# Reordering the first loads and the first turned weights of a two-layer graph kernel

## The chip, the core and the metric

The kernel runs on one core of one Trainium2 chip. Its time is the device time of one execution in microseconds (us). Three runs of the kernel before have a median of 1569.89 us (1569.67 to 1571.18). A separate, profiled execution gives the trace that is read here. The engines are called PE (the matrix engine), ACT (ScalarE), DVE (VectorE), POOL (GpSimd) and SP (the engine that issues most of the transfers).

## The reference, cut to what matters

Two layers work on x (4096 rows of 512 numbers) and an adjacency matrix of 4096 by 4096 with few ones.

```python
# layer 0
keep = (A > 0) & (cumsum(A > 0, axis=1) <= 64)
nb_mean = (keep @ x) / max(cnt, 1)
xj = leaky_relu(nb_mean @ W_nb.T + b_nb)
xi = leaky_relu(x @ W_line.T + b_line)
x = layernorm(x + xi + where(cnt > 0, xj, 0))
# layer 1
Wh = x @ W + bW
e = leaky(Wh @ a1 + b1 + (Wh @ a2 + b2).T);  e = where(A > 0, e, -9e15)
x = layernorm(x + softmax(e) @ Wh)
```

Only the two maps of layer 0, x by `W_nb` and x by `W_line`, and the folding of `W` with `a1` and `a2` have to do with the change.

## The kernel before

x is cut into 32 blocks of 128 rows. In layer 0 the kernel first makes the two maps of every block: `y = x @ W_nb.T`, which is stored in two parts, `y_hi` and `y_lo`, whose sum is y, and the line `x @ W_line.T + b_line`, which goes back to memory as `own_d`. Then one long loop (L723 to L750) multiplies the adjacency by all of y, and layer 1 follows (L1052 on). The order of the instructions on each engine is the order in which the program is written; each engine works through its own list, and a wait in it holds up everything behind it on that engine.

[...]both operands of a map have to be turned first. There are two ways of turning:

- `turn_by_pe` (L307) copies a 128 by 512 piece on DVE (L310) into one of four buffers `t`, lets PE turn it in four transposes (L153) into one of two PSUM buffers `pt`, and ACT copies the result to SBUF (L154). Block 0 of x and both weights go this way. A weight is turned in four parts of 128 of its output columns; part c fills columns 128c to 128c+127 of `w_t[name]`.
- Every other block of x is loaded by `load_turned_x` (L293) in four transfers on POOL's queue, with its 32 by 32 squares already in place, and DVE then turns each square (L325). The loads use three buffers `late[i % 3]`, so the load of block i + 3 waits for the turn of block i. The result lies in one of three `xt` buffers, or in room set aside for it.

`linear` (L368) makes one map of one block: four matmuls of 512 columns, each of which appears in the trace as two. `spin` (L353) issues transposes of the identity whose result nobody reads; they only keep PE busy.

The start of the program (L422 to L440) loads block 0 of x, the two weights, the line's bias, `W` and the rows `a1`, `a2`, `bW` on SP's queue, and two parts of `W_nb` on ACT's. It spins, turns block 0 and `W_nb`, makes the first map of block 0, turns `W_line`, makes the second map of block 0 and turns block 1 of x. From L494 the blocks come in pairs: sums and differences of the four pieces of the turned weights (`t1`, `t2`, `t4`, and `w12`, which is overwritten by `t3`) and of the turned x (`sums_x`) let `seven` (L533) make seven products instead of eight. Between the first map of block 0 and the first product of `seven` stand the steps that the prediction speaks of, in this order on DVE: the turn of block 2 (L494), `t1` and `t2` (L495, L496), the turn of block 3 into `x_low[1]`, a fourth `xt` buffer and so the one of block 0 again (L500), `y_low` of block 0 (L501), `line(0)` (L502), the sums (L508), `y_low` of block 1 (L510), `line(1)` (L512), `t4` and `t3` (L514, L515). ACT makes `y_hi` and the bend (Prelu) of each line, and before the loop of pairs it copies the bias into the PSUM bank of block 0's line (L589), into which the second product of the first `seven` adds.

The first `seven` (g = 1) also folds the weights: `fold_w` (L383) multiplies `W` and `bW` by the rows `a1` and `a2` and sums them, ten instructions on DVE spread over its four steps. From g = 2 on its steps hold the adjacency: `edge` on ACT (L175) and the scan on DVE (L193 to L206).

The buffers in which the raw weights are loaded are those in which the adjacency is worked on later: `nb` and `line` lie in the two `a` buffers, `W` in the two `left`, the rows in the two `edge`.

Of the kernel before, what the change touches and what calls it, by code (L numbers as in the profile page):

```python
# [9 lines left out]
F32 = mybir.dt.float32  # L10
# [10 lines left out]
P = 128  # L21
# [11 lines left out]
def two_layer_adj_gnn(  # L33
# [16 lines left out]
    nc = tc.nc  # L50
    N, C = x.shape
    NB = N // P
    NC = C // P
# [54 lines left out]
    late = [rows.tile([P, C], F32, name="c") for _ in range(3)]  # L108
# [28 lines left out]
    with ExitStack() as l0:  # L137
# [11 lines left out]
        def transpose_to(dst, src_of, n):  # L149

            pt = ps_s.tile([P, n, P], F32, name="pt")
            for k in range(n):
                nc.tensor.transpose(pt[:, k, :], src_of(k), ident)  # L153
            nc.scalar.copy(dst, pt)  # L154
# [128 lines left out]
        with ExitStack() as la:  # L283
            work = la.enter_context(tc.tile_pool(name="l0_work", bufs=2))
            wp = la.enter_context(tc.tile_pool(name="l0_w", bufs=1))
# [3 lines left out]
            w_t = {}  # L289
            xrs, xbs, xts, pys, pls = {}, {}, {}, {}, {}  # L290
            lines = {}

            def load_turned_x(i):  # L293

                if i < NB:
                    xrs[i] = late[i % 3].rearrange("p (j c) -> p j c", c=P)
                    for n in range(NC):
                        nc.gpsimd.dma_start(
                            xrs[i][ts(n, SQ)],
                            x_blk(i)[:, ts(n, P)].rearrange("(j a) c -> a j c", a=SQ),  # L300
                        )
# [5 lines left out]
            def turn_by_pe(dst, src):  # L307

                t = work.tile([P, C], F32, name="t", bufs=4)
                nc.vector.tensor_copy(  # L310
                    t.rearrange("p (m n b) -> p m n b", m=NC, b=SQ),
                    src.rearrange("p (n m b) -> p m n b", m=NC, b=SQ),
                )
                transpose_to(dst, lambda m: t[:, ts(m, P)], NC)

            def xt_tile():
                return work.tile([P, NC, P], F32, name="xt", bufs=3)

            def turn_x(i, t=None):
                if i < NB:  # L320
                    xts[i] = xt_tile() if t is None else t
                    if i == 0:
                        turn_by_pe(xts[i], xbs[i])
                    else:
                        nc.vector.transpose(  # L325
                            xts[i].rearrange("p m (j a) -> p j m a", a=SQ),
                            xrs.pop(i).rearrange("p j (m b) -> p j m b", b=SQ),
                        )
# [7 lines left out]
            raw = {}  # L336
# [12 lines left out]
            def load_w(name, src, queues):  # L349
                for c in range(NC):  # L350
                    queues[c % len(queues)].dma_start(raw[name][c], src[ts(c, P), :])

            def spin(n):  # L353

                idle = ps_acc.tile([P, P], F32, name="acc")
                for _ in range(n):
                    nc.tensor.transpose(idle, ident, ident)  # L357

            def turn_w(name, idle=0):

                wt = wp.tile([P, NC, C], F32, name=f"wt_{name}")
                for c in range(NC):
                    if idle:
                        spin(idle)
                    turn_by_pe(wt[:, :, ts(c, P)], raw[name][c])
                w_t[name] = wt

            def linear(lhs_t, name, bank=None):  # L368
                pl = ps_acc.tile([P, C], F32, name="acc") if bank is None else bank
                for k in range(NC):  # L370
                    nc.tensor.matmul(  # L371
                        pl, lhs_t[:, k, :], w_t[name][:, k, :],
                        start=(k == 0), stop=(k == NC - 1),
                    )
                return pl

            def load_rows(queue):
                for k, src in enumerate((a1, a2, b_w)):
                    queue.dma_start(early_rows[k], src.partition_broadcast(P))
                queue.dma_start(b12[:, 0:1], b1.partition_broadcast(P))  # L380
                queue.dma_start(b12[:, 1:2], b2.partition_broadcast(P))
# [33 lines left out]
            def y_terms(i, src):  # L415

                nc.scalar.copy(y_hi[i], src)
                return lambda: nc.vector.tensor_tensor(
                    y_lo[i], src, y_hi[i].bitcast(F32), ALU.subtract
                )  # L420

            load_own_x(0, nc.sync)  # L422
            load_w("nb", w_nb, (nc.scalar, nc.sync))
            load_turned_x(1)
            load_w("line", w_line, (nc.sync,))
            nc.sync.dma_start(bias_line, b_line.partition_broadcast(P))
            load_w("w", w, (nc.sync,))
            load_rows(nc.sync)
            load_turned_x(2)
            load_turned_x(3)  # L430
            spin(12)


            turn_x(0)
            turn_w("nb", 2)
            pys[0] = linear(xts[0], "nb")
            turn_w("line")
            pls[0] = linear(xts.pop(0), "line")
            turn_x(1)
            load_turned_x(4)  # L440

            wide = [pls[0]]

# [51 lines left out]
            tt(t1, w12, w11, ALU.subtract)  # L495
            tt(t2, w22, t1, ALU.subtract)  # L496
            y_low = y_terms(0, pys[0])
            pys[1] = linear(xts[1], "nb")
            x_low[1] = xt_tile()
            turn_pair(1, 1)  # L500
            y_low()  # L501
# [88 lines left out]
            idle = [lambda: None] * 4  # L590
# [80 lines left out]
        start = done[0]  # L671
# [51 lines left out]
        for s in range(NB * NS):  # L723
            i, g = divmod(s, NS)
# [14 lines left out]
            for k in range(KB):  # L739
                j = g * KB + k  # L740
                for term in (y_hi, y_lo):
                    nc.tensor.matmul(  # L742
                        accs[i], kt[:, k // 2, k % 2, :], term[j],
                        start=(j == 0 and term is y_hi),
                        stop=(j == NB - 1 and term is y_lo),
# [16 lines left out]
    wp = tile_p("l1_w", 3)  # L762
# [38 lines left out]
    x1ts, x1rows, pws, nats, wts, parts = {}, {}, {}, {}, {}, {}  # L801
# [232 lines left out]
    cnt, idle = cnts[:, 0, :], cnts[:, 1, :]  # L1034
# [17 lines left out]
    for s in range(NS):  # L1052
# [13 lines left out]
        k = s - FIRST  # L1066
# [13 lines left out]
        if s in range(FIRST + 14, FIRST + 22, 2):  # L1080
            q, part = divmod((s - FIRST - 14) // 2, 2)
# [5 lines left out]
    for q in range(NP * NT):  # L1087
        g, k = divmod(q, NP)
# [99 lines left out]
```

## Time and profile before

| | |
|---|---|
| median of three runs | 1569.89 us (1569.67 to 1571.18) |
| the profiled execution's own time | 1572.24 us |
| its span, first to last instruction | 1570.4 us |
| PE busy | 1559.4 us (99%) |
| DVE busy | 1258.5 us (80%) |
| ACT busy | 952.6 us (61%) |
| POOL busy | 241.2 us (15%) |
| first map's matmuls begin | 11.68 us into the span |
| first `seven`'s second product begins | 30.81 us into the span |

Times inside the profile are microseconds from the start of the span. A line of the chain of work reads: start, length, engine or transfer, tile and source line, count. A line of the timeline reads: start, length, engine, source line, operation, output and inputs, count, and in brackets how long the engine stood idle before and what ended that. L153 and L154 are the lines of a helper that every turned piece shares. A busy PE in the table counts matmuls whose ends are modelled.

### The profile page before, as it was taken

The page shows a single profiled execution, that of the slowest core. Times are in us where ns is not written, and L with a number is a line of the kernel's source. Part 1 is how long each engine was busy: PE and PEld are TensorE (multiplying, and loading weights), DVE is VectorE, ACT ScalarE, POOL GpSimd, SP SyncE. Part 2 cuts the span into 40 slices and gives each one's busy share as a digit, 9 for nine tenths or more (in the row PEclk, how much of TensorE's full clock was granted, in tenths as well). Part 3 has the DMA queues.
Part 4 walks back from the last instruction along what each step waited for, and adds up shares of the span by engine and source line. Part 5 has one row for each costly group of instructions (what it writes and reads, how often), then busy time and mean ns, then how long its engine had stood idle before and what let it go on. Part 6 is the DMA issues. An engine that isn't in the chain of part 4 may idle for free.

```text
span 1570.4 us, 18598 instructions
## 1 busy us (share of the span) xinstructions
PE 1559.4 (99%) x6408; PEld 1211.5 (77%) x6408; DVE 1258.5 (80%) x2306; ACT 952.6 (61%) x1123; POOL 241.2 (15%) x397
## 2 busy tenths in 40 slices
PE   8999999999999999999999999999999999999998
PEld 5444468888888888854488888888888888888887
DVE  5888658999999998447888888788878878888765
ACT  2676558887888878417065675556765557655530
POOL 4454212222122122120000000000000000000000
PEclk9999999999999999999999999999999999999999
DMA  7766468889888987653111111111111111111101
GB/s 234 201 203 208 160 166 265 258 250 258 242 260 222 265 253 209 147 120 113 50 41 41 28 54 53 43 48 27 48 54 41 54 34 35 55 41 54 42 1 40
DMA packets 170430, 193.01 MB, mean 123 GB/s; under 512 B 101424, under 2 KB 134480, under 8 KB 162144
## 3 DMA queue, kind: packets, MB, share of 16 engines
q1 hardware_dynamic: 147968, 131.38, 29.2%
q0 software_dynamic: 21792, 59.53, 13.3%
q8 instruction: 50, 0.82, 0.2%
q10 hardware_dynamic: 576, 0.92, 0.2%
q14 instruction: 44, 0.36, 0.1%
HBM read 132.91 MB, written 42.08 MB: 111 GB/s over the span
## 4 chain that ended last, share of the span: by engine, by line
PE 97%; DVE 1%; DMA 1%; ACT 0%; issue 0%; POOL 0%; POOLq 0%; DVEq 0%; ACTq 0%
PE acc L970 35%; PE acc L742 30%; PE pt L970 14%; PE acc L489 8%; PE acc L1056 7%; PE acc L371 3%; PE pt L371 0%; PE pt L153 0%; DMA c<-in_x_dram 0%; DVE edge L386 0%; DMA xb<-in_x_dram 0%; DVE left L194 0%; ACT edge L175 0%; PE acc L357 0%; ACT wt_line L154 0%
## 5 line engine op out<-in xcount | busy, mean ns | idle before, releaser
L970 PE MATMUL acc<-bt,s 128*128 128x256 f32 x1504 | 335.7, 379 | 0.0
L742 PE MATMUL acc<-y_hi,kt 128*128 128x512 f32 x824 | 320.5, 389 | 0.0
L742 PE MATMUL acc<-y_lo,kt 128*128 128x512 f32 x824 | 320.5, 389 | 0.0
L970 PEld LDWEIGHTS acc<-bt,s 128*128 128x128 f32 x1504 | 285.8, 190 | 38.9
L855 ACT ACTIVATE w<-nat,few 128x1024 f32<-128x1024 uint8 x128 | 136.9, 1137 | 293.3 <-DVE a L930 238.8
L970 PE MATMUL acc<-bt,a 128*128 128x256 f32 x1056 | 239.0, 379 | 0.0
L970 PE MATMUL pt<-bt,a 128*128 128x256 f32 x992 | 224.5, 379 | 0.0
L970 PEld LDWEIGHTS acc<-bt,a 128*128 128x128 f32 x1056 | 200.6, 190 | 27.3
L970 PEld LDWEIGHTS pt<-bt,a 128*128 128x128 f32 x992 | 188.5, 190 | 26.1 <-issue 0.5
L930 DVE STREAM_TRANSPOSE a<-w 128x1024 f32<-128x1024 f32 x128 | 153.1, 1225 | 62.0 <-ACT w L911 53.2
L277 ACT ACTIVATE kt<-ktb,few 128x1024 fp32r<-128x1024 uint8 x124 | 142.7, 1152 | 97.8 <-PE acc L742 80.1
L126 POOL TENSOR_TENSOR rs<-ve,few 128x1 f32<-128x1 f32 x64 | 46.8, 731 | 940.3 <-DVE ve L124 927.6
L742 PEld LDWEIGHTS acc<-y_lo,kt 128*128 128x128 f32 x824 | 154.7, 188 | 32.2
L742 PEld LDWEIGHTS acc<-y_hi,kt 128*128 128x128 f32 x824 | 154.6, 188 | 32.1
L848 ACT ACTIVATE w<-w,st_n 128x1024 f32<-128x1024 f32 x128 | 149.4, 1234 | 33.3 <-DVE m L865 33.3
L911 ACT ACTIVATE w<-w,nm 128x1024 f32<-128x1024 f32 x128 | 145.4, 1138 | 11.1 <-DVE nm L902 11.1
L865 DVE CUSTOM_DVE_ANT_0 w<-e_n,w 128x1024 f32<-128x1024 f32 x128 | 149.4, 1220 | 1.8 <-ACT w L855 0.5
L175 ACT ACTIVATE edge<-a,few 128x2048 bf16<-128x2048 int32 x64 | 136.2, 2128 | 6.3 <-issue 2.7
L223 ACT CAST code<-left 128x2048 uint8<-128x2048 bf16 x64 | 121.2, 1893 | 0.0
L1056 PE MATMUL acc<-w,c 128*128 128x512 f32 x232 | 99.7, 592 | 0.0
L1056 PEld LDWEIGHTS acc<-w,c 128*128 128x128 f32 x232 | 44.1, 190 | 55.5 <-issue 53.8
L206 DVE TENSOR_TENSOR left<-edge,left 128x2048 bf16<-128x2048 bf16 x64 | 78.4, 1225 | 2.2
(188 smaller groups left out, 1904.5 us busy)
## 6 DMA issues: line engine op xcount, KB each, us to landing
a<-in_adj_dram SPq DMA_DIRECT2D x64, 1024.0 KB, 5.9
code_d<-code POOLq DMA_DIRECT2D x64, 256.0 KB, 4.0
nat<-code_d SPq DMA_DIRECT2D x256, 64.0 KB, 2.0
w<-x_d SPq DMA_DIRECT2D x128, 64.0 KB, 2.0
c<-in_x_dram POOLq DMA_DIRECT2D x124, 64.0 KB, 5.2
own<-in_x_dram SPq DMA_DIRECT2D x31, 256.0 KB, 3.2
own<-own_d POOLq DMA_DIRECT2D x31, 256.0 KB, 5.5
x_d<-own POOLq DMA_DIRECT2D x31, 256.0 KB, 4.8
```

The costliest lines, as they stand in the source:

```text
L175: nc.scalar.activation(edge_of[s], loaded.pop(s).rearrange("p (t q) -> p q t", q=2), AF.Sigmoid, bias=steep[:, 0:1], scale=STEEP, accum_ou ...
L223: nc.scalar.copy(code.bitcast(U8).rearrange("p (t q) -> p q t", q=2), seen_of.pop(s))
L277: nc.scalar.activation(kts[s], bytes_.rearrange("p t (i r) -> p t r i", r=2), AF.Sigmoid, bias=steep[:, 1:2], scale=STEEP,)
L489: nc.tensor.matmul(bank, lhs[:, k, :], rhs[:, k, :], start=start and k == 0, stop=k == 1, skip_group_check=True,)
L742: nc.tensor.matmul(accs[i], kt[:, k // 2, k % 2, :], term[j], start=(j == 0 and term is y_hi), stop=(j == NB - 1 and term is y_lo),)
L848: nc.scalar.activation(dst, src, AF.Prelu, bias=bias, scale=scale, alpha=0.2)
L855: nc.scalar.activation(wts[b][:, i, :], nats[b, i // 2].bitcast(U8)[:, i % 2, :], AF.Relu, bias=far, scale=-FAR,)
L865: nc.vector.tensor_tensor_reduce(w_i, e2_n, w_i, 1.0, -3e38, ALU.subtract, ALU.max, m4s[b][:, i : i + 1])
L911: nc.scalar.activation(w_i, w_i, AF.Exp, bias=nms[b][:, i : i + 1], accum_out=z4s[g][:, r, i : i + 1])
L930: nc.vector.transpose(a[:, r].rearrange("p s (i a) -> p i s a", a=SQ), wts[2 * g + r][:, :, ts(k, 8 * SQ)].rearrange("p i (s x) -> p i s x ...
L970: nc.tensor.matmul(banks[g][n], lhs[:, j, :], bt[:, 4 * k + j, rhs, :], start=(k == 0 and j == 0 and n == mate[0]), stop=(k == NP - 1 and ...
L1056: nc.tensor.matmul(pws[s], x1t[:, m, :], ws[:, m, :], start=(m == 0), stop=(m == NC - 1))
```

## The change

The order of the first loads changes. Block 1 of x moves from POOL's queue to SP's, between `W_nb` and `W_line`. `W_line` is issued by ACT and SP in turn, as `W_nb` was. Blocks 2 and 3 of x, and `W` with the rows, are issued later in the program, each group behind a memset on DVE that writes one column of its first buffer: the transfer writes the same column and so has to wait for the memset, and the memset stands on DVE behind the copies of `W_nb`, or behind the turn of block 1. There are 15 spins ahead of the first turn instead of 12.

The first map of block 0 is made in two pieces: columns 0 to 383 first, columns 384 to 511 after two parts of `W_line` have been turned. Both pieces add into the same PSUM bank. Then the other two parts of `W_line` are turned. After that comes the map of block 1 by `nb`, and only then the map of block 0 by `line`. Before, block 0's `line` map came first, and block 1's `nb` map stood after `t1`, `t2` and `y_terms(0, ...)` in the program.

```diff
-            def load_turned_x(i):
+            def load_turned_x(i, queue=nc.gpsimd):
...
-                        nc.gpsimd.dma_start(
+                        queue.dma_start(
...
-            def turn_w(name, idle=0):
-
-                wt = wp.tile([P, NC, C], F32, name=f"wt_{name}")
-                for c in range(NC):
+            def turn_w(name, idle=0, parts=range(NC)):
+
+                if name not in w_t:
+                    w_t[name] = wp.tile([P, NC, C], F32, name=f"wt_{name}")
+                for c in parts:
                     if idle:
                         spin(idle)
-                    turn_by_pe(wt[:, :, ts(c, P)], raw[name][c])
-                w_t[name] = wt
-
-            def linear(lhs_t, name, bank=None):
+                    turn_by_pe(w_t[name][:, :, ts(c, P)], raw[name][c])
+
+            def linear(lhs_t, name, bank=None, part=slice(0, C)):
+
                 pl = ps_acc.tile([P, C], F32, name="acc") if bank is None else bank
                 for k in range(NC):
                     nc.tensor.matmul(
-                        pl, lhs_t[:, k, :], w_t[name][:, k, :],
-                        start=(k == 0), stop=(k == NC - 1),
+                        pl[:, part], lhs_t[:, k, :], w_t[name][:, k, part],
+                        start=(k == 0 and part.start == 0),
+                        stop=(k == NC - 1 and part.stop == C),
+                        skip_group_check=part.stop - part.start < C,
                     )
                 return pl
...
             load_own_x(0, nc.sync)
             load_w("nb", w_nb, (nc.scalar, nc.sync))
-            load_turned_x(1)
-            load_w("line", w_line, (nc.sync,))
+            load_turned_x(1, nc.sync)
+            load_w("line", w_line, (nc.scalar, nc.sync))
             nc.sync.dma_start(bias_line, b_line.partition_broadcast(P))
+            spin(15)
+
+
+            turn_x(0)
+            turn_w("nb", 2)
+
+            for i in (2, 3):
+                nc.vector.memset(late[i % 3][:, 0:1], 0.0)
+                load_turned_x(i)
+            pys[0] = linear(xts[0], "nb", part=slice(0, 3 * P))
+            turn_w("line", 0, range(0, 2))
+            linear(xts[0], "nb", pys[0], slice(3 * P, C))
+            turn_w("line", 0, range(2, 4))
+            turn_x(1)
+            load_turned_x(4)
+            nc.vector.memset(raw["w"][0][:, 0:1], 0.0)
             load_w("w", w, (nc.sync,))
             load_rows(nc.sync)
-            load_turned_x(2)
-            load_turned_x(3)
-            spin(12)
-
-
-            turn_x(0)
-            turn_w("nb", 2)
-            pys[0] = linear(xts[0], "nb")
-            turn_w("line")
+            pys[1] = linear(xts[1], "nb")
             pls[0] = linear(xts.pop(0), "line")
-            turn_x(1)
-            load_turned_x(4)
...
             y_low = y_terms(0, pys[0])
-            pys[1] = linear(xts[1], "nb")
             x_low[1] = xt_tile()
```

## The prediction

> **What bounds the kernel now.** First the page's chain of work that ended last, by engine:
>
> ```profile
> PE 97%; DVE 1%; DMA 1%; ACT 0%; issue 0%; POOL 0%; POOLq 0%; DVEq 0%; ACTq 0%
> ```
>
> The matrix engine (PE) is nearly the whole chain, so only its idle stretches can be won or lost. The chain in order of time says where they are:
>
> ```profile
> 51.34 122.27 PE acc L489 x284
> ```
>
> From 51.34 us on PE runs without a gap, so what the change does before that comes out as a shift of all that follows. I then read the chain of the first 56 us:
>
> ```profile
> 0.74 3.74 DMA xb<-in_x_dram
> ...
> 10.37 0.64 PE pt L153 x4
> 11.02 0.02 issue
> 11.04 0.59 ACT wt_nb L154
> 11.63 0.04 issue
> 11.68 3.70 PE acc L371 x8
> ...
> 17.18 1.09 ACT wt_line L154 x2
> 18.27 0.04 issue
> 18.31 3.71 PE acc L371 x8
> 22.02 0.02 issue
> 22.05 0.72 DVE xt L325
> ...
> 50.67 0.62 DVE acc L574
> 51.29 0.04 issue
> ```
>
> Block 0 of x (`xb`) lands at 4.48; the turn of `nb` runs on PE to 11.0. Twice PE then stands until ScalarE (ACT) has copied the last turned part of a weight, 0.67 us before 11.68 and 0.68 before 18.31. From 22.05 VectorE (DVE) carries the chain. The chain shows a DMA of x at 24.68 to 29.48, but the instruction behind it (L514) reads no x and stands directly behind L402 on DVE, so I take that step for a coincidence. The timeline gives the rest:
>
> ```profile
> 1.37 2.82 PE L357 MATMUL acc<-ident 128*128 128x128 f32 x12 [1.37 <-POOL ident masks.py:199]
> 4.99 1.12 PE L153 MATMUL pt<-ident,t 128*128 128x128 f32 x4 [0.80 <-DVE t L310]
> 15.21 1.04 PE L153 MATMUL pt<-ident,t 128*128 128x128 f32 x8
> 28.91 0.69 DVE L402 TENSOR_TENSOR t<-acc,bias_line 128x512 f32<-128x512 f32 x1 [2.12 <-PE acc L371]
> 30.81 3.70 PE L489 MATMUL acc<-hi,lo 128*128 128x512 f32 x8 [0.22 <-ACT acc L589]
> ```
>
> L402 at 28.91 is `line(1)`, the bias added to the second map of block 1. It waits for PE. Behind it DVE works without a pause to 42.9, then comes the first `edge` on ACT and its scan, up to the product at 51.34. So **the start of line(1) sets 51.34**, and with it the end.
>
> **The change, part by part.**
>
> Loads up to the first map. ACT issues four transfers instead of two. At 0.45 each (two took 0.90) they end near 2.6; its table load (1.28) then ends near 3.9 instead of 2.95, under the wait for the first copy at 6.14. Price 0; if ACT's issues had to wait, each us past a table end of 6.1 would be lost. SP issues `xb`, two parts of `nb`, four of x block 1, then `line` parts 1 and 3, bias. SP's seventh issue before (4.68) stood until `xb` had landed at 4.48, so `line` part 3, ninth in its queue, goes out near 5.9. The data up to it is 2.62 MB; 0.56 MB came before 4.0 us and 335 GB/s followed from 4 to 8, so it lands near 10.2 (before: 13.1). The last `nb` part landed at 7.37 (issue 1.67, 5.7 to landing). Its new neighbour on the engines is a part of `line` instead of x from POOL; even at 8.5 it stays ahead of its turn near 9.7. Price 0.
>
> Three more spins: at the pitch of the cold turn, 0.2133 (four take 0.85), they end at 4.19 + 0.64 = 4.83, before the first turn at 4.99. Price 0.
>
> [...]The clock column shows 1.00 in all these windows, so I read the rate from durations: four transposes take 0.85 from 5 to 10 us, eight take 1.04 at 15.21, and the x4 at 10.37 takes 0.64, that is two at 0.213 and two at 0.107. Full rate began near 10.8. [...] The longer spin cuts the 0.80 gap to 0.16. [...] I take 0, the nearer row, and keep 1.7 as a rival.
>
> The interleaving. Before, PE's way from the turn of `nb` to line(1): first matmul at 11.68, `pls[0]` ends 22.02. After, the first three quarters of block 0's map need only turned parts 0 to 2, and the third was copied by 10.57, so PE goes on at about 10.95. A 512-column matmul has two records 0.43 apart, so eight at 3/4 length take 2.58: 13.53. Two parts of `line` turned, 8 transposes at 0.107: 14.39. The last quarter, 8 records of 128 columns: between 0.107 (columns alone, or the transposes' pitch) and 0.190 (if the weight load of 190 ns cannot overlap); I take 0.115, near the transposes, whose loads overlap too: 0.92, 15.31 (bounds 0.86 and 1.52). Two more parts: 16.17; their PSUM buffers are free, since copies of 0.59 follow transposes that ended at 13.96 and 14.39. Then block 1 by `nb`, 3.44: 19.61, which covers the copy of the last `line` part (PE waited 0.68 for it before). Then block 0 by `line`: 23.05, with 0.26 of drain 23.3.
>
> This is 1.3 **later** than 22.02, and it matters: the turn of block 3 into `x_low[1]` takes the third-next `xt` buffer, that of block 0, and waits for this map. From that turn's start to line(1) DVE needs, by the starts before, 0.63 + 0.58 + 0.60 (turn, y_low, line(0)), three sums to 3.01, and 0.69 for y_low(1), plus about 0.1 as ACT's conversion for it ends 3.1 after the turn's start: 3.8. So line(1) starts at 27.1. PE ends the fourth map at 23.05 + 3.44 + 0.26 = 26.75 and is no longer what it waits for. Gain 28.91 − 27.1 = **1.8** (1.2 to 1.9 by the bounds of the last quarter). PE follows: 1.90 lay between line(1) and the product at 30.81 (bias, Prelu and a copy on ACT), so 29.0.
>
> Moved loads. Two memsets on DVE behind the last `nb` copy (7.9) release POOL at 8.1 for x blocks 2 and 3: 8 issues of 0.55, last at 12.0, at most 7.5 us to landing for such before: 19.5. Block 3 is wanted at 23.3; cover 3.8. Block 2 lands near 16.5, ahead of `t1`, which needs `line` copied near 16.9. Blocks 4 and 5 queue on POOL behind them and their own turns: landed by 27, wanted at 30 and 32. Block 6 goes out 1.3 later than at 23.05, landing near 30.8, wanted at 42.81 − 1.8. The third memset, behind the turn of block 1 (12.2), releases SP for `w`, the rows, then adjacency. That is 6.3 later than 5.93: a2 landed at 19.35, now 25.7, and the first fold wants it at 32.42 − 1.8 = 30.6; cover 4.9. Adjacency 0 landed at 27.1, now 33.4, wanted at 43.1. The memsets cost some 0.1 in DVE time where it waits anyway. All 0 while the covers hold.
>
> **Sum.** The profiled execution: 1572.24 (span 1570.4 and 1.84 around it) − 1.8 = 1570.4. The runs' median is 1569.89; the same shift gives **1568.1**.
>
> **Rivals.**
>
> A. As summed: 1568.1, own range 1567.4 to 1569.0. Chance 0.52.
>
> B. [...]1568.1 − 1.7 = 1566.4, with 1565.7 to 1567.2. [...] DVE and loads would follow: block 3 would be wanted at 21.6, `line` part 3 near 13. Chance 0.26.
>
> C. The gain is hidden: x block 3 lands late. Its landing at 23.3 + 1.8 would bring line(1) back to 28.91: 1569.9. A time of 10.9 to landing, the longest of its kind, gives 22.9, so it needs a slower one still, beside `w` and rows released in the same us. Or the chain at 24.68 was real after all. Chance 0.14.
>
> D. Slower: the fold weights come too late. DVE reaches the first fold at 30.6 with everything of the chain behind it. Up to 4.9 of lateness is covered; the next 1.8 eat the gain; to be slower by 3.1 takes a2 landing after 35.5, 23 us after the release instead of 13.4. With twice the old 13.4 it lands at 39.1, DVE stands 8.5, and the time is 1576.6. For it: these ten transfers now start together with x blocks 2 to 5. Against: `line` is done by then, and before they shared the engines with it. Chance 0.08.
>
> **How the numbers follow.** 0.2% is 3.1 us, about what this kernel's measurement can tell. Faster by more needs a time under 1566.75: about three quarters of B and 0.02 from elsewhere, 0.22. Slower: most of D and a remainder, 0.07. The rest, 0.71, is within. The range 1565.9 to 1570.5 holds A, nearly all of B and most of C, and leaves out D.
>
> **What would show it.** Right: no wait of PE for ACT between 11 and 18; the map of block 1 by `nb` ahead of block 0 by `line`; line(1) near 27.1 waiting for no PE; the unbroken run of PE from near 49.5. B: the transposes of `nb` part 2 at 0.107 apart. C: the turn of block 3 waits for a DMA. D: a fold waits for a DMA near 30.6. Wrong in a way not listed: the quarter of 128 columns takes over 1.5, or ACT's first copy is later than 6.14.

## The result, and the profile after

The changed kernel takes 1567.92 us (median of 14 runs, 1567.17 to 1568.77); 14 runs of the kernel before beside it take 1571.37 (1569.67 to 1572.42). The ratio is 0.998, with a 95% interval of 0.9972 to 0.9988: faster by 0.2%, 3.1 us by the ratio and 3.45 by the medians. The forecast time, 1568.1, is close, and the forecast range holds the measured one, but the forecast started from three runs with a median of 1569.89, lower than that of the 14. The gain is nearly twice the 1.8 us of the sum.

The page's chain of work by engine, of the kernel after:

```profile
PE 98%; DVE 1%; issue 0%; ACT 0%; DMA 0%; POOLq 0%; DVEq 0%; ACTq 0%
```

The chain of the first 56 us, of the kernel after (start, length, engine, tile and line; `linear` is L372 now, the products of `seven` are L498):

```profile
...
6.50 0.85 PE pt L153 x4
7.35 0.32 PE acc L357 x2
7.67 0.44 PE pt L153 x4
...
8.76 0.22 PE acc L357 x2
8.98 0.46 PE pt L153 x4
9.44 2.85 PE acc L372 x8
12.29 0.87 PE pt L153 x8
13.16 0.89 PE acc L372 x8
14.05 0.87 PE pt L153 x8
14.93 6.88 PE acc L372 x16
21.81 0.02 issue
21.83 0.71 DVE xt L325
...
47.26 0.62 DVE acc L582
47.88 0.04 issue
```

Both waits of PE for ACT are gone: from the turn of `nb` to the end of block 0's `line` map no other engine stands in the chain. The long chain of the same kernel:

```profile
47.92 122.15 PE acc L498 x284
```

The unbroken run starts at 47.92 instead of 51.34. The timeline of the kernel after:

```profile
1.37 3.46 PE L357 MATMUL acc<-ident 128*128 128x128 f32 x15 [1.37 <-POOL ident masks.py:199]
4.95 1.12 PE L153 MATMUL pt<-ident,t 128*128 128x128 f32 x4
...
7.51 0.60 PE L153 MATMUL pt<-ident,t 128*128 128x128 f32 x4
...
25.50 0.68 DVE L405 TENSOR_TENSOR t<-acc,bias_line 128x512 f32<-128x512 f32 x1
...
25.64 1.98 PE L498 MATMUL acc<-wt_nb,xt 128*128 128x512 f32 x4 [0.41 <-DVE y_lo L421]
```

The spins now reach almost to the first turn, and from near 7.4 us the transposes of `nb` take half the time (in the chain above four take 0.85 at 6.50 and 0.44 at 7.67). So PE's first map starts at 9.44. In the profile before the turn ended at 11.0 and the map started at 11.68. `line(1)` (now L405) has no wait in its row and starts at 25.50 instead of 28.91.

The accounts of the two profiled executions agree. Span 1570.4 to 1566.6 is 3.8. Of this, 3.41 is there at line(1): 11.0 − 9.44 = 1.56 from the clock, as PE's rate, read from these durations, is called below, and 1.85 from the order. The run of PE starts 3.42 earlier; its last matmul ends 3.57 earlier (1562.48 and 1558.91 in the chains), and the last transfer brings the other 0.2.

### The profile page after: what moved, and what is told of

Read it like the earlier page. It is cut to its first block, busy times and chain, and to the rows that moved or that the text cites. A ratio compares the mean times of both kernels' runs of the same rounds, so it can differ in the third digit from the quotient of the medians.

```text
span 1566.6 us, 18624 instructions
## 1 busy us (share of the span) xinstructions
PE 1557.8 (99%) x6419; PEld 1211.5 (77%) x6419; DVE 1258.2 (80%) x2309; ACT 952.7 (61%) x1123; POOL 238.4 (15%) x393
## 4 chain that ended last, share of the span: by engine, by line
PE 98%; DVE 1%; issue 0%; ACT 0%; DMA 0%; POOLq 0%; DVEq 0%; ACTq 0%
PE acc L978 35%; PE acc L750 30%; PE pt L978 14%; PE acc L498 8%; PE acc L1064 7%; PE acc L372 3%; PE pt L372 0%; PE pt L153 0%; DVE edge L389 0%; DMA xb<-in_x_dram 0%; DVE left L194 0%; ACT edge L175 0%; DVE y_lo L421 0%; DVE xt L325 0%; ACT L175 0%
```

## The experiments

All times are medians. Each group of four ran on one chip beside the kernel before, which took 1572.43 in the first group, 1572.48 in the second and 1572.76 in the third. That is 1.1 to 1.4 above the runs of the result, for changed kernel and old alike. So I compare differences to the before of the same group.

### Theories

Theory 1: the order of turns and maps gives 1.8 us and the clock, through the spins, the rest. Its rivals: the order gives all and the spins do nothing; or the loads are the gain.

### 1. The kernel before with 15 spins

```diff
-            spin(12)
+            spin(15)
```

> The kernel before with 15 spins in place of 12, nothing else. Theory 1 (the clock): of the 3.45 us between the medians 1571.37 and 1567.92 some 1.7 are the clock, which opened near 7.4 us in the changed kernel's profile and near 10.7 in the profile before; the three spins close the gap of 0.8 us ahead of the first turn and alone bring this. Then this kernel takes about 1569.8, and its second and later nb turns run at a pitch of 0.107 us. Rival (the order alone): [...]the spins do nothing, and this kernel takes 1571.4, as before.

1571.15, which is 1.28 under before (ratio 0.9993, 0.9985 to 1.0001). The interval just includes no change; the spread says more. All 13 executions lie within 1570.93 to 1571.72, while the 57 of before lie between 1570.28 and 1573.56. The timeline of this kernel shows the turn of `nb` at the full pitch from its first part, four transposes in 0.60 (1.06 at 6.33 in the profile before):

```profile
6.27 0.60 PE L153 MATMUL pt<-ident,t 128*128 128x128 f32 x4
...
27.03 0.69 DVE L402 TENSOR_TENSOR t<-acc,bias_line 128x512 f32<-128x512 f32 x1 [2.13 <-PE acc L371]
```

line(1) still waits 2.13 for PE, as before, and starts 1.88 earlier than there. The expected 1.6 is not reached in the median, perhaps because some executions of before reach the full rate early too; none of them was profiled, so this is not shown (experiment 2 has such an execution of the changed kernel).

### 2. The changed kernel with 12 spins

```diff
-            spin(15)
+            spin(12)
```

> The changed kernel with the 12 spins of before. Theory 1 (the clock): the gap of 0.8 us is back, [...]and 1.2 to 1.7 us of the gain go: about 1569.4. Rival (the order alone): 1567.9, unchanged.

1570.06, 2.37 under before (0.9987, 0.998 to 0.9993). The 21 executions fall into two groups with nothing between: 8 from 1568.37 to 1569.14, 13 from 1569.97 to 1571.18. Their medians, 1568.67 and 1570.51, lie 1.84 apart, near the 1.7 that the prediction left to rival B. The profiled one took 1568.47, so it is of the quicker group, and its timeline fits that:

```profile
5.04 0.66 PE L153 MATMUL pt<-ident,t 128*128 128x128 f32 x4 [0.84 <-DVE t L310]
5.53 0.38 PE L357 MATMUL acc<-ident 128*128 128x128 f32 x2
5.75 0.60 PE L153 MATMUL pt<-ident,t 128*128 128x128 f32 x4
```

The gap of 0.84 is there, and still the first turn runs at full rate (four transposes in 0.66, 1.12 in the profile before). No execution of the slower group was profiled, so that it reaches the full rate later is inferred from the 1.84. The profile before, and that of experiment 4, have the same 12 spins and a gap of 0.80 and 0.81, and full rate only behind 10 us (four still take 1.06 at 8.88 and at 8.90): with 12 spins both were seen. So the spins alone do not decide it, but the rival was wrong that they do nothing. The ten profiles with 15 spins in this document, that of the kernel after among them, all have full rate by 7.5 (0.60 to 0.63 for four in the rows behind it), though in some of them the first turn comes late and the gap is as long as 0.50 (experiment 1).

### 3. The old order of the maps in the changed kernel

```diff
-            pys[1] = linear(xts[1], "nb")
             pls[0] = linear(xts.pop(0), "line")
...
             y_low = y_terms(0, pys[0])
+            pys[1] = linear(xts[1], "nb")
```

> The changed kernel with block 0's line map ahead of block 1's nb map again, and the latter behind t1 and t2 in the program, as before. Theory 1: PE waits some 0.68 us for the copy of the last line part, so the fourth map ends near 25.9 instead of 25.25, line(1) then waits for PE again and starts near 26.0 instead of 25.5: 0.4 to 0.5 us slower than the changed kernel, 1568.4. Rival (the turn of block 3, which now waits for block 0's line map, is what sets line(1), so the old order is better): 1567.0 to 1567.5.

1569.5, 2.93 under before (0.998, 0.9973 to 0.9987), against 3.21 for the changed kernel in the second group (experiment 5): 0.3 dearer, where theory 1 had 0.4 to 0.5. The row of its timeline where the cover is gone, and that of line(1):

```profile
15.58 1.98 PE L372 MATMUL acc<-wt_line,xt 128*128 128x512 f32 x4 [0.73 <-ACT wt_line L154]
...
26.18 0.69 DVE L405 TENSOR_TENSOR t<-acc,bias_line 128x512 f32<-128x512 f32 x1 [2.13 <-PE acc L372]
```

PE waits 0.73 for the last copy. The turn of block 3 comes earlier in return, but line(1) waits for PE again. It starts 16.82 behind the start of the first map (9.36 here), against 16.06 in the profile after, so 0.76 is lost up to there. The medians show less, and their difference is too small to tell from none by these intervals; the rows are what shows the mechanism.

### 4. The new loads alone, in the kernel before

```diff
-            load_turned_x(1)
-            load_w("line", w_line, (nc.sync,))
+            load_turned_x(1, nc.sync)
+            load_w("line", w_line, (nc.scalar, nc.sync))
...
-            load_w("w", w, (nc.sync,))
-            load_rows(nc.sync)
-            load_turned_x(2)
-            load_turned_x(3)
...
+            for i in (2, 3):
+                nc.vector.memset(late[i % 3][:, 0:1], 0.0)
+                load_turned_x(i)
...
+            nc.vector.memset(raw["w"][0][:, 0:1], 0.0)
+            load_w("w", w, (nc.sync,))
+            load_rows(nc.sync)
```

> The kernel before with the new loads alone: block 1 of x on SP, line on ACT and SP, blocks 2 and 3 and the fold weights behind memsets; 12 spins and the old order of turns and maps. Theory 1: line was copied by 13.65 and first wanted on PE at 15.2, so earlier loads bring nothing by themselves: 1571.4, within 0.3. Rival (the loads are the gain, as less traffic lands with the first weights): 1569 or less.

1572.58, 0.15 over before (1.0001, 0.9993 to 1.0009). By themselves the loads bring nothing.

### 5. The changed kernel once more

> The changed kernel unchanged, beside the next three and the kernel before. Theory 1 (order 1.8, clock 1.3 to 1.7): 3.1 to 3.5 us under the before of the same call. Rival [...]: 1.8 to 2.4 under.

1569.27, 3.21 under before (0.9981, 0.9973 to 0.999). The gain of the result is there again. The higher level comes, at least in part, from a load of the adjacency. The rows of the third `edge` on ACT, first in the profile after, then in that of this run, here with PE's wait behind it:

```profile
54.55 2.16 ACT L175 ACTIVATE edge<-a,few 128x2048 bf16<-128x2048 int32 x1 [1.84 <-DMA a<-in_adj_dram]
```

```profile
55.16 2.16 ACT L175 ACTIVATE edge<-a,few 128x2048 bf16<-128x2048 int32 x1 [3.42 <-DMA a<-in_adj_dram]
...
60.33 1.98 PE L498 MATMUL acc<-wt_line,lo 128*128 128x512 f32 x4 [1.10 <-DVE acc L582]
```

This load is issued when the first `edge` is done, at 43.71 there and at 42.74 here, so it took longer here, and PE waits 1.10 behind it. The profiles of experiments 1 to 8 are all like this one: the load takes 11.7 to 12.4 us from its issue, and the run of PE without a gap begins 5.2 us after the third `edge` begins. In the profiles before and after the load takes 11.2 and 10.8, and PE does not wait. Being tied to the first `edge`, the load passes on every gain ahead of it, but its own time differs from profile to profile by more than some of the differences below.

### 6. The first map in one piece

```diff
-            pys[0] = linear(xts[0], "nb", part=slice(0, 3 * P))
+            pys[0] = linear(xts[0], "nb")
             turn_w("line", 0, range(0, 2))
-            linear(xts[0], "nb", pys[0], slice(3 * P, C))
             turn_w("line", 0, range(2, 4))
```

> The changed kernel with block 0's first map in one piece ahead of all four turns of line. Theory 1: PE waits for the copy of the last nb part again, some 0.6 to 0.7 us as in the profile before; the rest follows 0.6 to 0.7 later, so 0.6 to 0.7 over the changed kernel. Rival (PE has slack there because DVE's chain from the turn of block 3 sets line(1)): 0 to 0.2.

1570.35, 2.13 under before (0.9987, 0.9981 to 0.9994): 1.1 over the changed kernel, where 0.6 to 0.7 was expected. Its timeline shows a second wait that I had left out:

```profile
9.47 3.70 PE L372 MATMUL acc<-wt_nb,xt 128*128 128x512 f32 x8 [0.68 <-ACT wt_nb L154]
...
14.28 1.14 PE L153 MATMUL pt<-ident,t 128*128 128x128 f32 x8 [0.24 <-ACT wt_line L154]
```

Four turns in a row need two PSUM buffers twice, and PE stands 0.24 for the copy that frees one. Together 0.92; line(1) starts 1.15 later behind the end of the turn of `nb` than in the profile after (17.21 and 16.06). The last quarter of the map, put between the turns, covers this wait as well as the first.

### 7. The old loads in the changed kernel

```diff
-            load_turned_x(1, nc.sync)
-            load_w("line", w_line, (nc.scalar, nc.sync))
+            load_turned_x(1)
+            load_w("line", w_line, (nc.sync,))
             nc.sync.dma_start(bias_line, b_line.partition_broadcast(P))
+            load_w("w", w, (nc.sync,))
+            load_rows(nc.sync)
+            load_turned_x(2)
+            load_turned_x(3)
```

The memsets go too, and with them the later loads behind them.

> The changed kernel's order of turns and maps and its 15 spins, but all loads as before (block 1 of x on POOL, line on SP alone, fold weights and blocks 2 and 3 at once, no memsets). Theory 1: line part 3 landed at 13.1 before and PE would take it near 14.3, so the loads are just in time: 0 to 0.3 over the changed kernel. Rival (the new order lives by the earlier line): PE waits for line parts 2 and 3, 1 us or more over the changed kernel.

1569.93, 2.55 under before (0.9986, 0.9979 to 0.9993): 0.66 over the changed kernel, between the two expectations. In its profile the `line` parts land just in time: DVE waits for the last until 13.84, and PE takes it without a wait of its own. line(1) starts 16.12 behind the start of the first map, 16.06 in the profile after, so this profile does not show where 0.66 goes. That execution did not have the earliest clock (two spins take 0.63 at 6.22 and 0.38 only from 7.49); with PE a us further ahead the cover would be gone. That part is argued, not shown.

### 8. Twenty spins

```diff
-            spin(15)
+            spin(20)
```

> The changed kernel with 20 spins. At the half rate of 0.2133 they end at 5.64, 0.7 after the first turn could begin. Theory 1 (the gap is what mattered, and 15 spins leave 0.12 of it): [...]the later turn costs 0.35 to 0.7: 1568.3 to 1568.6 where the changed kernel takes 1567.9. Rival (the more spins the sooner the clock): as fast or faster, by up to 0.5.

1569.25, 3.23 under before (0.9979, 0.9971 to 0.9987), the same as with 15. Theory 1's loss is not there, nor any gain; the rival's "as fast" is what was measured. In its profile the first turn is at full rate at 5.39 (four transposes in 0.66). How an earlier clock and a later start balance over the executions I cannot tell from one profile.

### 9 to 11. What is left on DVE's chain

```diff
             tt(t2, w22, t1, ALU.subtract)
+            tt(t4, w21, t2, ALU.subtract)
...
-            tt(t4, w21, t2, ALU.subtract)
```

> The changed kernel with t4 made directly behind t2, where DVE stood 3.7 us, instead of behind line(1). Theory 1 (DVE's chain from line(1) sets the start of the unbroken run of PE): 1.13 us less in that chain, of which PE can use its idle 0.28, 0.14 and 0.59 between 34 and 48 us: 0.8 to 1.0 under the changed kernel, 1568.3 where it took 1569.27. Rival (PE or the loads bind there): 0 to 0.2 under.

1568.13 (six runs), 4.63 under before (0.9969, 0.9957 to 0.9981): 1.4 further than the changed kernel in the second group, where 0.8 to 1.0 was expected, and by the medians faster than both kernels. Against before the interval leaves no doubt; against the changed kernel, which ran in another group, the two intervals overlap. Its timeline has t4 (L506) in DVE's old pause, and t3 (L523) directly behind line(1), and from line(1) to the first `edge` it takes 14.81 instead of 15.95, 1.14 less where 1.13 was expected:

```profile
18.01 1.23 DVE L506 TENSOR_TENSOR hi<-wt_nb,hi 128x1024 f32<-128x1024 f32 x1
21.69 0.71 DVE L325 STREAM_TRANSPOSE xt<-c 128x512 f32<-128x512 f32 x1 [2.46 <-PE acc L372]
...
25.36 0.68 DVE L405 TENSOR_TENSOR t<-acc,bias_line 128x512 f32<-128x512 f32 x1
25.96 1.22 DVE L523 TENSOR_TENSOR wt_line<-wt_line 128x1024 f32<-128x1024 f32 x1
```

In the profile after t4 began at 26.10, behind line(1) in DVE's list, although `t2` was done by 18.11 (16.89 + 1.22) and DVE stood 3.72 for PE before 21.83: that wait held it up, as it held all behind it.

Then block 3 turned into free room, alone and with the edit above:

```diff
-            x_low[1] = xt_tile()
+            x_low[1] = halves(room_lo[:, 5])
```

> The changed kernel with block 3 turned into free room instead of the xt buffer of block 0, so that the turn waits for no map. Theory 1: line(1) then waits for PE, 0.2 earlier than with the changed kernel, and the first product no longer waits for y_low of block 1 (0.41 there): 0.2 to 0.3 under the changed kernel. Rival (the turn of block 3 is the bound as such): 0.7 or more under.

1569.1, 3.66 under before (0.9978, 0.9971 to 0.9985): 0.45 further, a little over the expected 0.2 to 0.3. But this kernel and the next spend 2.1 us outside the span, where every other kernel here spends 1.8; by the median spans the gain is 0.8, as the rival had it. In its profile line(1) starts 15.82 behind the start of the first map, 16.06 in the profile after: that part is the expected one. What the rest is, and the 2.1, stays open.

> Both edits of the last two together on the changed kernel. Theory 1: the sum, limited by PE's idle time between 25 and 48 us, 1.45 in all: 1.1 to 1.4 under the changed kernel, near 1568.0 where it took 1569.27, and faster than both kernels. Rival: 0 to 0.5 under.

1568.12 (eight runs), 4.64 under before (0.9972, 0.9962 to 0.9982). As expected in size, but by its time no further than the first edit alone; by the spans it is 0.35 further. That DVE's chain behind line(1) passes its length on to the end is shown by the edit of t4; the order of these two kernels is not resolved by so few runs.

### 12. The fold weights at once

```diff
             nc.sync.dma_start(bias_line, b_line.partition_broadcast(P))
+            load_w("w", w, (nc.sync,))
+            load_rows(nc.sync)
             spin(15)
...
-            nc.vector.memset(raw["w"][0][:, 0:1], 0.0)
-            load_w("w", w, (nc.sync,))
-            load_rows(nc.sync)
```

> The changed kernel with W and the rows issued directly behind the line's bias, as before, without the third memset; the rest of the new loads stays. Theory 1 (holding them back only moves hidden traffic): 0 to 0.2 over the changed kernel. Rival (the 0.66 that the old loads cost is this traffic beside line's parts): 0.4 to 0.7 over.

1569.91, 2.85 under before (0.9983, 0.9976 to 0.9989). Set against their befores, the changed kernel is 0.4 better (3.21), by the plain medians 0.64: nearer to the rival. The turn of block 2 in this kernel's timeline, and from its table of waits PE's wait for `y_low` (us in total, times, longest):

```profile
18.59 0.71 DVE L325 STREAM_TRANSPOSE xt<-c 128x512 f32<-128x512 f32 x1 [5.28 <-DMA c<-in_x_dram]
```

```profile
PE acc L497 <- DVE y_lo L421: 1.2, 1, 1.2
```

Block 2 of x lands at 18.6, at 13.57 in the profile after, with `W` and the rows beside it on the transfer engines. DVE gets to t1, t2 and the turn of block 3 that much later, and PE, early by its clock, waits 1.2 for `y_low`. line(1) starts 16.84 behind the start of the first map, 16.06 in the profile after. This execution was among the slowest of the 20 (1571.07), so it shows how the loss comes about, and more of it than the median has. As far as this goes, the third memset earns its place not by what it loads but by what it lets pass.

## Why the prediction was right or wrong

**What sets the end: right, with a load left out.** The start of line(1) moved by 3.41 and the unbroken run by 3.42, and an edit that only shortens DVE's work behind line(1) moved the end. But where the third load of the adjacency takes longer, as in the profiles of experiments 1 to 8, PE waits for it too before its run begins (experiment 5). The prediction had no term for it.

**The interleaving: right, and right in size.** From the start of the first map to the end of block 0's `line` map the sum had 10.95 to 23.3, 12.35 us; the profile has 9.44 to 21.81, 12.37. The last quarter took 0.89 of the chosen 0.92. From there to line(1) it was 3.69 of the forecast 3.8. PE ended its fourth map before DVE was ready, as said, and waited 0.41 for `y_low`.

**The clock: the step that failed.** The sum took 0, "the nearer row", and left 1.7, which no row of the profile before shows, to rival B, an earlier full rate. In the profile it was 1.56. Experiments 1 and 2 give it as 1.28 and 0.84 in the medians, less than 1.56, as one would expect if 12 spins too are followed by an early full rate at times, as in the profile of experiment 2. The row leaned on, a gap of 0.80 and half rate until near 10.8, did not speak of a gap of 0.12 (4.83 to 4.95 in the profile after). Rival B described the execution. In gain the medians, 3.1 to 3.45, are near B's 3.5 and not near A's 1.8.

**The covers of the moved loads: right for what was moved late, wrong for what was left out.** ACT's copies, the memsets and the fold weights cost nothing, and no wait showed where rivals C and D had put theirs. But the new loads were priced at 0, and in the changed order they are worth 0.66 by the medians (experiment 7; nothing in the old order, experiment 4). The covers were summed for the late clock only; rival B named the earlier times but no price. With PE 1.5 us ahead, block 2 can set the pace, as experiment 12 shows for one execution; that the last `line` part would do so as well is argued. One time of issue was also wrong: `line` part 3 went out at 7.57, not near 5.9, since SP's fifth transfer already stood until 4.64. It was still copied by 11.4, well before PE turned it near 14.

**The median it started from.** The three runs had 1569.89, the 14 have 1571.37. The start that was too low by 1.5 and the gain that was too small by 1.3 to 1.65 cancel in the forecast time. That it came so near is luck.

## What to carry to other kernels

An idle stretch ahead of the first real work on PE cost more than its length here: a gap of 0.8 us, with PE still at half rate, went with a loss of 1.56 in the profiles and 1.28 in the medians of experiment 1, though in the profile of experiment 2 full rate followed a gap of 0.84. Read the rate from the duration of equal instructions, not from the clock column: it shows 1.00 in the profile before from 5 to 10 us, where four transposes of the chain take 0.85, and in the profile after from 7.5 to 9.4, where they take 0.44 to 0.46. Let the spins reach the first real instruction, or nearly (0.12 us short of it in the profile after). Look for a copy on the way from one PE step to the next and put independent PE work of at least its length there, a part of a split map included. And cost a moved load at the earliest time at which the sped-up engine may want it, not at the time of the old profile.

## What was not expected of the hardware

With 12 spins the full rate starts early or late: in experiment 2 the spins, which end at 4.19, are followed by four transposes in 0.66 at 5.04, while in the profile before the same 12 spins, 2.82 us of PE from 1.37 and so with the same end, are followed by half rate until about 10.8. The two groups of 8 and 13 executions in experiment 2 would fit this, one for each start, but only the quicker has a profile, and what decides it is not shown. And the same adjacency load of 1 MB landed 12.4 us behind its issue in the fifth experiment and 10.8 in the profile after. What made the difference is open; both kernels stood over 1 us higher there, and their difference was nearly the same (3.21, and 3.45 in the result).
